# A four-layer model with routed experts on one core: where the first ranks' rows are added, and in which order layer 3's shared expert runs

## The chip, the cores and the metric

The kernel runs on one core of a Trainium2 chip. Five engines work from their own instruction queues: PE (matrix multiply), DVE (vector), ACT (scalar functions), POOL (general purpose) and SP (which here only issues transfers). They wait for each other with semaphores, and each executes its own queue in order. DMA queues move data between HBM and the on-chip memory. The metric is the device time of one execution in microseconds; the number quoted is a median over runs.

## The reference

The model has 1,024 tokens of width 256 (2 sequences of 512) in fp32 and four layers. Each layer is "macaron" shaped: half a feed-forward block, an attention-like block, half a feed-forward block. Layer 0 uses retention attention, layer 1 attention over selected tokens, layers 2 and 3 Mamba-2 blocks. The feed-forward blocks of layers 0 and 3 are mixtures of experts, and these are what the change touches:

```python
scores = softmax(x2d @ wg_router.T)                 # layer 3: sigmoid
topk_w, topk_idx = top_k(scores, TOP_K)             # layer 0: 6 of 32, layer 3: 2 of 8
...                                                 # layer 0: an expert takes at most C tokens
ye = (silu(xe @ w_gate) * (xe @ w_up)) @ w_down     # each expert on its tokens, F = 176
y = sum over the TOP_K ranks of ye * weight
sh = (silu(x2d @ ws_gate) * (x2d @ ws_up)) @ ws_down   # shared expert, on all tokens
return y + sh
```

Each token's result is a sum over its K chosen experts, plus the shared expert, plus the residual. Both blocks are run twice, before and after the layer's attention.

## The kernel before, in words

The tokens live on chip as `x`, eight chunks of 128 tokens (partitions) by 256. All four layers are one program. A tile framework places each engine's instructions by dependences; in some stretches the order is written out by hand with `in_order` (L230), which ties every instruction of the named engines to the one traced before it. `warm` (L254-259) issues PE matmuls whose result nobody reads, to fill PE's waits.

`moe` does a routed block. Its route (normalised tokens, router logits) may have been started by the stage in front; class `Route` has a method for each step (`measure`, `centre`, `turn`, `logit`, `load`, `clear`, `store`). Then:

- `choose` finds the top K experts of every token on DVE. `slots` (L531) gives each token a slot at each expert: a prefix count over tokens on PE (`ps_pos`, L540-541), then integer work on DVE (`sl_full` to `sl_hl`). `slot_lists` turns slots into two lists of row numbers, with one-hot tiles on DVE (L581-584) and PE, ended by a step `meet`: `sl_get` (which token to gather) and `sl_put` (where a result row goes).
- `shared_unit` (L472) runs the shared expert for one half of the tokens at a time: `front` multiplies by gate and up (L483), ACT makes silu, DVE multiplies (`h`, L487), `back` multiplies by down into `acc` (L493), and DVE adds `acc` to `x`. Layer 0 has three blocks of its hidden width, layer 3 two of 88.
- `experts_sparse` (L622) loops over experts in tiles of slots, software-pipelined over units: SP loads an expert's weights (L635-637) into one of five buffers of the pool `weights`; POOL gathers token rows (L645); PE transposes them (L661), multiplies by gate and up (L673); ACT and DVE form `he` (L677-678); PE transposes (L687), DVE or ACT copies to `hT`, PE multiplies by down (L698), DVE or ACT copies to `ye`, and POOL scatters `ye` to the array `rows` in HBM (L704). `rows` has K rows for every token, one for each rank; ranks follow the number of the expert, so a token's rank-0 row belongs to its first expert. A slot list hence fills rank 0 only from experts up to E-K, rank 1 only up to E-K+1, and so on.
- An overflow flag `over` decides whether further tiles are needed. All engines load it and branch around an `If` (L837-839); in these runs the body is not executed.
- After the `If`, every chunk needs its K rows. SP fetches them (L861) once all scatters have landed. `add` sums them: with a PSUM pool given, PE adds the K rows with identity matmuls (L879) and DVE adds the result (L880); else, for K=6, DVE adds rows 3-5 to rows 0-2 (L883, 128x768) and then three rows to `x` (L886); for K=2 two L886. These are not done by `moe` itself but left `pending` per chunk, and the stage that comes next calls `settle` (L261) for each chunk when it needs it. In layer 0's attention the order is written by hand, with `early_rows` making a chunk's addition fetch rows for the other half; in layer 1's front odd chunks of the first half and all of the second use PSUM.

Layer 3's routing is prepared in the stage in front: `l2_ffn2` ahead of its first routed block, the Mamba stage (steps near its end, from `NS - 7` on) ahead of its second.

Of the kernel before, what the change touches and what calls it, by code (L numbers as in the profile page):

```python
# [18 lines left out]
P = 128  # L19
# [82 lines left out]
class Route:  # L102

    def __init__(self, net, sb, xT, xn, pre, names, E, F, K, FS, PER, tiles, cap, r, scores, scale):
        self.net, self.sb, self.xT, self.xn = net, sb, xT, xn
        self.xns = [xn[c // CB][:, c % CB, :] for c in range(NC)]
        self.E, self.K, self.cap, self.r, self.scores = E, K, cap, r, scores
        a = net.a
# [10 lines left out]
        self.blocks, self.scales = None, {}  # L119
# [8 lines left out]
    def clear(self):  # L128
        nc = self.net.nc
        zero = self.sb.tile([P, D], F32, name="zero")  # L130
        nc.gpsimd.memset(zero, 0.0)
        for c in range(NC):
            nc.sync.dma_start(self.rv[c, :, : self.K, :], zero.unsqueeze(1).to_broadcast([P, self.K, D]))
# [38 lines left out]
    def store(self, b, engine):  # L172
        engine.dma_start(self.tv[b], self.xn[b])


class Net:
# [295 lines left out]
    def shared_unit(self, work, psA, psM, xT, blocks, half, scale):  # L472

        nc = self.nc
        cols = slice(half * S, (half + 1) * S)
        acc = [psA.tile([P, 2, D], F32, tag="acc", name=f"acc{i}") for i in range(2)]

        def front(gv, uv, bw):
            pg = psM.tile([P, S], F32, tag="mm", name="pg")
            pu = psM.tile([P, S], F32, tag="mm", name="pu")  # L480
            for ps, wv in ((pg, gv), (pu, uv)):
                for k in range(KD):
                    nc.tensor.matmul(ps[:bw], wv[:, k, :], xT[:, k, cols], start=(k == 0), stop=(k == KD - 1))  # L483
            s = work.tile([P, S], F32, tag="s", name="s")
            h = work.tile([P, S], F32, tag="h", name="h")
            nc.scalar.activation(s[:bw], pg[:bw], AF.Silu)
            nc.vector.scalar_tensor_tensor(h[:bw], s[:bw], scale, pu[:bw], ALU.mult, ALU.mult)  # L487
            return h

        def back(h, dv, bw, first, last):  # L490
            for tc_ in range(CB):

                nc.tensor.matmul(  # L493
                    acc[tc_ // 2][:, tc_ % 2, :],
                    h[:bw, tc_ * P : (tc_ + 1) * P],
                    dv,
                    start=first and tc_ % 2 == 0,
                    stop=last,
                    skip_group_check=True,
                )  # L500

# [247 lines left out]
    def moe(self, pre, names, E, F, K, FS, PER, tiles, cap, r, scores, scale):  # L749
# [6 lines left out]
        with ExitStack() as es:  # L756
# [4 lines left out]
            with ExitStack() as fs:  # L761
# [46 lines left out]
                for f in parts:  # L808
                    f()
# [1728 lines left out]
```

## Time and profile before

| quantity | us |
|---|---|
| median of 3 runs | 1982.44 (1980.68 to 1988.79) |
| the profiled execution, its own time | 1985.63 |
| its span | 1983.8 |
| PE busy | 1763.2 (89%) |
| DVE busy | 1148.7 (58%) |
| ACT busy | 817.4 (41%) |
| POOL busy | 924.2 (47%) |

The stages in the trace, in us from the start of the span: layer 0's first FFN 0-265, its attention 265-444, its second FFN 444-686; layer 1 686-869; layer 2 869-1140; layer 3's first FFN 1140-1250, its Mamba block 1250-1850, its second FFN 1850-1984.

A line of a timeline gives the start, the duration, the engine, the program line, the operation with the tiles it writes and reads, and in brackets how long the engine had been idle and who released it. A line of a table of windows gives the window, its length, and the busy time of PE, PE's weight loads, DVE, ACT and POOL in it, with instruction counts; then PE's granted clock, the share of DMA and the GB/s moved. An instruction of PE in fp32 appears as two pieces.

### The profile page before, as it was taken

The numbers are of one execution on the slowest core, as the hardware profiler recorded it, in microseconds if no ns is written. First come the engines' busy times: TensorE is split into PE (matmuls) and PEld (weight loads), VectorE is DVE, ScalarE is ACT, GpSimd is POOL, SyncE is SP. The second block draws the span as 40 slices with busy tenths as digits, with TensorE's granted clock in tenths as the row PEclk, the third lists the DMA queues.
The fourth block names the chain that finished last, engine by engine and source line by source line (L and its number), as shares of the span: only waits on it lengthen the run. The fifth ranks groups of instructions, "written<-read, shape, count | busy, mean of one in ns | idle before, by whom it ended". The sixth has DMA issues, their size and how long they took to land. (4 is left out here: it accounts for less than half of the span.)

```text
span 1983.8 us, 29591 instructions
## 1 busy us (share of the span) xinstructions
PE 1763.2 (89%) x10370; PEld 1249.3 (63%) x10370; DVE 1148.7 (58%) x2963; ACT 817.4 (41%) x1430; POOL 924.2 (47%) x946
## 2 busy tenths in 40 slices
PE   7988989998898887889788988789999999999985
PEld 4666766665666665554465456557777777777663
DVE  5422348346332367666676743578777877778523
ACT  1122225421222214421662112278877777777221
POOL 3556546522656440120142135136656656767362
PEclk8999999999999998999899999899999999999897
DMA  8355551052545360010130022534454544544132
GB/s 275 111 185 153 152 186 66 2 171 58 158 139 152 98 214 1 1 43 0 76 108 23 11 64 77 171 103 147 155 169 159 156 146 157 168 147 134 39 102 90
DMA packets 122216, 226.55 MB, mean 114 GB/s; under 512 B 22414, under 2 KB 75004, under 8 KB 121910
## 3 DMA queue, kind: packets, MB, share of 16 engines
q1 hardware_dynamic: 97062, 179.08, 27.9%
q0 software_dynamic: 18944, 42.16, 7.0%
q10 hardware_dynamic: 6032, 3.10, 0.6%
q8 instruction: 92, 1.51, 0.3%
q14 instruction: 86, 0.70, 0.1%
HBM read 195.59 MB, written 41.81 MB: 120 GB/s over the span
## 5 line engine op out<-in xcount | busy, mean ns | idle before, releaser
L645 POOL DMA_INDIRECT xe<-table,sl_get x176 | 181.0, 1029 | 206.3 <-DVE sl_get L617 96.6
L704 POOL DMA_INDIRECT rows<-ye,sl_put x176 | 176.8, 1004 | 126.4 <-DVE ye L225 40.9
L673 PE MATMUL ps_gu<-we,xeT 128*128 128x352 f32 x704 | 231.1, 470 | 1.6 <-DVE xeT L225 1.5
L698 PE MATMUL ps_ye<-we,hT 88*128 88x256 f32 x704 | 178.1, 395 | 38.6 <-issue 16.9
L698 PEld LDWEIGHTS ps_ye<-we,hT 88*128 88x128 f32 x704 | 135.0, 195 | 83.7 <-issue 20.4
L2066 DVE SCALAR_TENSOR_TENSOR xc<-pp,L_attn_cols,xc 128x511 f32<-128x511 f32 (+2 forms) x216 | 161.5, 748 | 26.2 <-ACT xc L2062 20.9
L678 DVE SCALAR_TENSOR_TENSOR he<-se,xe,ps_gu 128x176 f32<-128x176 f32 x176 | 68.3, 396 | 172.4 <-ACT se L677 93.5
L673 PEld LDWEIGHTS ps_gu<-we,xeT 128*128 128x128 f32 x704 | 129.7, 196 | 59.1 <-issue 4.8
L2181 DVE SCALAR_TENSOR_TENSOR lm<-lm,jb,top 128x128 f32<-128x128 f32 x576 | 153.6, 342 | 0.0
L2290 PE MATMUL yacc<-wt,y 128*128 128x256 f32 x576 | 142.7, 391 | 0.6 <-DVE x L2308 0.3
L2260 POOL TENSOR_TENSOR y<-y,sg 128x512 f32<-128x512 f32 x72 | 91.8, 1275 | 104.9 <-DVE y L2259 101.7
L677 ACT ACTIVATE se<-ps_gu 128x176 f32<-128x176 f32 x176 | 54.1, 318 | 204.7 <-PE ps_gu L673 117.9
L2205 PE MATMUL pz<-lateT,wt 128*128 128x128 f32 x1024 | 125.7, 276 | 6.2 <-ACT xt L2154 4.1
L2198 POOL TENSOR_TENSOR ce<-ce,CT 128x1024 f32<-128x1024 f32 x54 | 128.0, 2370 | 0.0
L2205 PEld LDWEIGHTS pz<-lateT,wt 128*128 128x128 f32 x1024 | 119.7, 192 | 9.3 <-ACT xt L2154 5.3
L2059 PE MATMUL pp<-lateT,wx 128*128 128x512 f32 x256 | 123.4, 605 | 1.4 <-DVE jb L2045 0.6
L1833 PE MATMUL ps_y<-w8T,xT 128*128 128x512 f32 x256 | 123.2, 610 | 0.0
L2233 PE MATMUL py<-lm,xt 128*64 128x128 f32 x1152 | 108.1, 281 | 14.4 <-ACT xc L2062 4.7
L2290 PEld LDWEIGHTS yacc<-wt,y 128*128 128x128 f32 x576 | 103.8, 190 | 22.7 <-issue 8.9
L2190 DVE TENSOR_TENSOR lm<-lm,M 128x1024 f32<-128x1024 f32 x72 | 87.2, 1215 | 45.6 <-ACT lm L2186 43.1
L2271 POOL TENSOR_TENSOR sqs<-sqs,sq 128x512 f32<-128x512 f32 x56 | 71.3, 1274 | 84.3 <-ACT sq L2270 84.3
L2221 POOL TENSOR_TENSOR xd<-xt,dec 128x512 f32<-128x512 f32 x54 | 56.4, 1044 | 93.5 <-ACT xt L2154 93.5
(510 smaller groups left out, 3562.6 us busy)
## 6 DMA issues: line engine op xcount, KB each, us to landing
lm<-rows SPq DMA_DIRECT2D x72, 512.0 KB
ce<-rows SPq DMA_DIRECT2D x54, 512.0 KB
y<-rows SPq DMA_DIRECT2D x16, 768.0 KB
we<-in_L_ffn_w_gate_dram SPq DMA_DIRECT2D x64, 176.0 KB
we<-in_L_ffn_w_up_dram SPq DMA_DIRECT2D x64, 176.0 KB
we<-in_L_ffn_w_down_dram SPq DMA_DIRECT2D x64, 176.0 KB
we<-in_L_ffn_w_dram SPq DMA_DIRECT2D x48, 176.0 KB
wx<-in_L_attn_in_proj_w_dram SPq DMA_DIRECT2D x16, 512.0 KB
```

The source lines that it names most:

```text
L645: nc.gpsimd.indirect_dma_start(xe[:, i, :], None, table, bass.IndirectOffsetOnAxis(get[:, at + j : at + j + 1], 0), bounds_check=T - 1, oo ...
L673: nc.tensor.matmul(pg, xeT[:, k, i * P : (i + 1) * P], wgu[:, :, k], start=(k == 0), stop=(k == KD - 1))
L698: nc.tensor.matmul(py[:, i, :], hT[:, q, i * P : (i + 1) * P], wd[:, q, :], start=(q == 0), stop=(q == 1))
L704: put_rows = nc.gpsimd.indirect_dma_start(rows, bass.IndirectOffsetOnAxis(put[:, at + j : at + j + 1], 0), y[:, i, :], None, bounds_check= ...
L1833: nc.tensor.matmul(ps, xT[:, k, :], self.w8T[:, k, 2 * e2 : 2 * e2 + 2, :], start=(k == 0), stop=(k == KD - 1))
L2059: nc.tensor.matmul(pp, wv[:, k, :], xT[:, k, b * S : (b + 1) * S], start=(k == 0), stop=(k == KD - 1))
L2066: nc.vector.scalar_tensor_tensor(out[:, 3 - w :], pp[:, : S - 3 + w], cw[:, m, w : w + 1], out[:, 3 - w :], ALU.mult, ALU.add)
L2181: nc.vector.scalar_tensor_tensor(k["lm"][:, h, :], k["lm"][:, h, :], jb[:, k["c"], n : n + 1], top, ALU.add, ALU.min)
L2198: nc.gpsimd.tensor_tensor(k["ce"], k["ce"], ct, ALU.mult)
L2205: nc.tensor.matmul(pz[:, m, :], u["wz"][:, kk, m * P : (m + 1) * P], xT[:, kk, c * P : (c + 1) * P], start=(kk == 0), stop=(kk == KD - 1),)
L2233: nc.tensor.matmul(py[i * HP : (i + 1) * HP, m, :], w[:, h * HP : (h + 1) * HP], v[:, h, :], start=(m == 0 and n == 0), stop=(n == len(src ...
L2290: nc.tensor.matmul(yacc[cc // 2][:, cc % 2, :], k["y"][:, m, :], u["wo"][:, m, :], start=(u["g"] == 0 and m == 0 and cc % 2 == 0), stop=(u ...
```

## The change

It has four parts.

1. **First ranks' rows are summed beside the last experts.** `early` is 4 of 6 ranks in layer 0, 1 of 2 in layer 3. When expert E-K+j is through (`done`), `take(j)` loads all tokens' rank-j rows (1 MB, in 1 KB pieces) by SP: rank 0 into a tile `sums` from the weight pool, later ranks into a single-buffered tile `yr`, which four DVE additions of 128x512 add to `sums`. Later scatters are declared independent of these loads, since later experts hold only higher ranks. After the `If`, four DVE additions of 128x512 add `sums` to `x`; the pending additions then fetch and add only the K-early last ranks. `early_rows` goes. L879 then runs for 2 rows instead of 6, L883 is gone.
2. **Rank 0 may now be read where nothing was scattered**, so for layer 3 `clear` is now called too, when the route is loaded: it writes zeros to the first rank's rows, in eight stores on SP, from a tile of zeros that POOL sets. The tile `latec` grows from 720 to 944 columns.
3. **The shared expert becomes a class `Shared`**, whose hidden tile `hs` is one buffer of the weight pool. Layer 3's front of half 0, block 0, is issued at the end of the stage in front (before the last chunk's `route_turn` in `l2_ffn2`; after `add_row` in the Mamba stage, with the shared weights loaded some steps before). Its second front takes the place of four warm matmuls in the second call, and stands behind `choose` in the first.
4. **Layer 3's lists get a fixed order** on PE and DVE: choose, slots (with the weighing of scores, `weigh`, between the prefix count's issue and `sl_full`), back and front of the next block, the list steps, two products `h`, `meet`, and then the rest of the shared expert.

The instruction order of the changed kernel, as built, puts the four additions of `take(1)` on DVE between the two `he` tiles of expert 30 in both calls of layer 0; those of `take(2)` and `take(3)` follow the last `hT`.

```diff
+        self.early = K - max(1, K // 3)
...
     def clear(self):
         nc = self.net.nc
+        n = self.K if self.cap < T else self.early
...
+            nc.sync.dma_start(self.rv[c, :, :n, :], zero.unsqueeze(1).to_broadcast([P, n, D]))
...
+class Shared:
+    def __init__(self, net, xT, blocks, scale):
+        self.hs = net.w("hs")[:, : B * len(blocks) * S].rearrange("p (b n t) -> p b n t", b=B, n=len(blocks))
+    def front(self, b, n, psum, pool, tag="s"):
...
+        nc.scalar.activation(s[:bw], pg[:bw], AF.Silu)
+        return partial(
+            nc.vector.scalar_tensor_tensor, self.hs[:bw, b, n, :], s[:bw], self.scale, pu[:bw], ALU.mult, ALU.mult
+        )
...
+                for other in self.taken:
+                    self.tc.declare_no_dep(put_rows.ins, other, reason="lower ranks than this expert can have")
                 self.puts.append(put_rows)
+            if done and js[-1] == tiles[-1]:
+                done(e)
...
-                        if left:
+                        if left and not route.shared_ahead:
                             self.warm(psM, 4)
+                        elif left:
+                            second = route.shared_ahead.front(0, 1, psM, work)
...
+                if shared:
+                    with self.in_order(tail, ("PE", "DVE")):
+                        for b in range(B):
+                            route.choose(b)
+                        if not left:
+                            second = shared.front(0, 1, psM, work)
+                        hl, row, full = self.slots(lists, sb, psL, mask, E, cap, r, weigh)
+                        shared.back(0, 0, psA)
+                        third = shared.front(1, 0, psM, work)
+                        where, parts = lists_of()
+                        for f in parts[:-1]:
+                            f()
+                        second()
+                        third()
+                        parts[-1]()
+                        third = shared.front(1, 1, psM, work)
+                        shared.back(0, 1, psA)
+                        shared.sum(0)
+                        third()
+                        for n in range(2):
+                            shared.back(1, n, psA)
+                        shared.sum(1)
...
+                def take(j):
+                    if j == 0:
+                        t = sums["of"]
+                    else:
+                        t = ew.tile([P, NC, D], F32, name="yr")
+                    nc.sync.dma_start(t, tv[j])
+                    self.taken.append(self.last_on("SP"))
+                    for c in range(0, NC if j else 0, 2):
+                        ac = sums["of"][:, c : c + 2, :]
+                        nc.vector.tensor_tensor(ac, ac, t[:, c : c + 2, :], ALU.add)
+
+                def done(e):
+                    j = e - (E - K)
+                    if j == 0:
+                        sums["of"] = self.w("sums")[:, : NC * D].rearrange("p (c d) -> p c d", d=D)
+                    if 0 <= j < early:
+                        take(j)
...
+        for c in range(0, NC, 2):
+            xc = self.x[:, c : c + 2, :]
+            nc.vector.tensor_tensor(xc, xc, sums["of"][:, c : c + 2, :], ALU.add)
...
         def add_rows(b, cc, psum):
+            n = K - early
+            for r in range(B):
+                if r not in ys and (r == b or cc == 0):
+                    ys[r] = self.w("y2")[:, : CB * n * D].rearrange("p (c n d) -> p c n d", c=CB, n=n)
+                    for i in range(CB):
+                        nc.sync.dma_start(ys[r][:, i], route.rv[r * CB + i, :, early:K, :])
+            y, xc = ys[b][:, cc], self.x[:, b * CB + cc, :]
+            if psum and n > 1:
...
             with self.in_order(tail, ("PE",)):
+                if route:
+                    shared.front(0, 0, psM, st)()
                 route_turn(NC - 1)
                 route_logit(NC - 1)
...
+                def begin():
+                    route.load()
+                    route.clear()
+                    route.shared_ahead = Shared(self, xT, self.load_shared(*route.shared), 0.5)
...
+            with self.in_order(tail):
+                project(ks.pop(NS - 1))
+                add_row(B - 1)
+                if not few:
+                    route.shared_ahead.front(0, 0, psM, wk, "sq")()
```

## The prediction

> **What bounds the kernel now.** I read the page's busy table first, then the stretches in which the diff acts, one at a time, in the timeline and the table of windows. The page:
>
> ```profile
> span 1983.8 us, 29591 instructions
> PE 1763.2 (89%) x10370; PEld 1249.3 (63%) x10370; DVE 1148.7 (58%) x2963; ACT 817.4 (41%) x1430; POOL 924.2 (47%) x946
> ```
>
> PE is busy for 89%, but this includes keep-warm matmuls, so a stage is judged by what it waits for. The change acts in six places: the two exits of layer 0's routed FFN (255-345, 670-735), the two heads of layer 3's (1138-1175, 1850-1887) and their two exits (1250-1264, 1966-1984). The first exit, on DVE (start, duration, instruction, idle before and its releaser):
>
> ```profile
> 254.58 0.40 DVE L678 SCALAR_TENSOR_TENSOR he<-se,xe,ps_gu 128x176 f32<-128x176 f32 x1 [0.85 <-ACT se L677]
> 255.76 0.40 DVE L678 SCALAR_TENSOR_TENSOR he<-se,xe,ps_gu 128x176 f32<-128x176 f32 x1 [0.79 <-issue]
> ...
> 262.12 0.69 DVE L225 COPY hT<-ps_he 88x512 f32<-88x512 f32 x1 [1.42 <-PE ps_he L687]
> 276.99 0.96 DVE L883 TENSOR_TENSOR y<-y 128x768 f32<-128x768 f32 x1 [14.18 <-DMA y<-rows]
> 277.98 1.34 DVE L886 TENSOR_TENSOR x<-x,y 128x256 f32<-128x256 f32 x3
> ```
>
> DVE is done with the experts at 262.8 and idles 14.18 us, until rows come back from HBM. Then every 128-token chunk costs a L883 and three L886, until 337. By then DVE is full (window, then busy PE, PEld, DVE, ACT, POOL):
>
> ```profile
> 310.00:321.00 11.00, 10.04 (x108) 7.24 (x107) 9.98 (x24) 5.59 (x16) 8.01 (x9) 1.00 0.25 77
> 321.00:332.00 11.00, 10.15 (x102) 6.68 (x101) 10.47 (x26) 6.41 (x19) 8.34 (x9) 1.00 0.08 26
> 332.00:343.00 11.00, 10.99 (x111) 7.62 (x110) 9.93 (x24) 5.11 (x16) 7.79 (x9) 1.00 0.17 51
> ```
>
> Layer 3's first head, on PE:
>
> ```profile
> 1142.69 0.69 PE L148 MATMUL pt_r<-cst,laten 128*128 128x128 f32 x2 [4.49 <-DVE laten L307]
> 1143.84 1.02 PE L154 MATMUL ps_lg<-latec,lateT 128*128 128x8 f32 x4 [0.46 <-ACT lateT L149]
> 1145.12 3.71 PE L483 MATMUL pg<-lateT,wsh 128*88 128x512 f32 x4 [0.26 <-DVE latec L157]
> 1148.63 2.82 PE L483 MATMUL pu<-lateT,wsh 128*88 128x512 f32 x4
> 1151.28 1.02 PE L483 MATMUL pg<-lateT,wsh 128*88 128x512 f32 x2
> 1152.14 0.34 PE L540 MATMUL ps_pos<-sl_pre,cst 128*128 128x72 f32 x2
> ```
>
> PE idles 4.49 us, runs cold afterwards (0.85 us a piece; granted clock 0.50 in 1145-1150), and reaches the slot count (ps_pos) at 1152.14, behind ten shared-expert pieces, though DVE had its input by 1148.1. The last exit, on DVE:
>
> ```profile
> 1969.25 1.68 DVE L886 TENSOR_TENSOR x<-x,y 128x256 f32<-128x256 f32 x4 [10.16 <-DMA y<-rows]
> 1971.61 0.89 DVE L886 TENSOR_TENSOR x<-x,y 128x256 f32<-128x256 f32 x2 [0.69 <-DMA y<-rows]
> 1972.70 1.68 DVE L886 TENSOR_TENSOR x<-x,y 128x256 f32<-128x256 f32 x4 [0.20 <-DMA y<-rows]
> 1975.89 0.88 DVE L886 TENSOR_TENSOR x<-x,y 128x256 f32<-128x256 f32 x2 [1.50 <-DMA y<-rows]
> 1978.68 1.68 DVE L886 TENSOR_TENSOR x<-x,y 128x256 f32<-128x256 f32 x4 [1.91 <-DMA y<-rows]
> ```
>
> 6.8 us of adds take 11.1 us, because fetches reuse buffers and stand behind output stores on SP.
>
> **First exit of layer 0.** Added: four takes of 1 MB in 1 KB pieces, 12 adds of 128x512 into sums, 4 into x. An add is taken at 0.69 us (L883 moves 768 columns in 0.96), four at 2.8. A take: attention weights of the same piece size moved at about 345 GB/s (250-253), so 3.0 us, plus some 2 for start and landing (a 256 KB row fetch issued at 1252.14 let DVE start at 1254.83): 5.0. Bounds: 3.0 (transfer alone) to 7.
>
> In the changed instruction order DVE meets the first four adds between expert 30's two he tiles, and they need take 1. That take waits for expert 27's second scatter (issued 249.29; its packets end by 252-253) and lands at about 257.5; the adds end at 260.4, so the he of 255.76 starts 4.6 us late. Queued behind it are he and hT of experts 30 and 31, and behind those PE's down projections and POOL's last four scatters, whose last (267.06) goes about 2 us late, because PE now runs expert 31's gate/up inside the gap. All takes after the first share one buffer yr: take 2 runs 260.5-265.5, its adds end at 268.3; take 3 lands at 273.4, its adds end at 276.2. Then DVE reads the overflow flag, branches and fetches code: before, its branch stood at 262.76 and its next record at 265.62, which cost nothing ahead of the 14 us wait; now these 3.4 us are in the chain: 279.6. Four adds into x: 282.4; two row adds: chunk 0 is complete at 283.2 rather than 279.3. The row fetch itself (landing near 277-278) is hidden behind this chain. So +3.9 at the start.
>
> [...]
>
> Chunks 0 to 7 lose L883 (8.4 us in this window) and a third of L886 (15.3): 13.5 us of DVE, of which 2.3 belong to chunks 0 and 1 and are returned at once, the rest in steps where DVE is 9.9-10.5 of 11 busy, but PE 10.0-11.0 too. Ends: 0 (PE bounds) and 11.2 (DVE alone). I take 6, since PE's busy time includes cold and modelled ends. Sum: +3.9 -2.3 -6 = **-4** (range +4 to -9). SP's five weight loads move from 247 to behind take 1 (253); first used after 283, so free.
>
> **Second exit, and layer 1's front.** The same chain: take 1 lands at 676, adds to 678.5, he late by 3.6, last scatter +0.8; take 2's adds 685.8, take 3's 693, branch 696.4, adds into x 699.2, chunk 0 at 700.0, against 698.7: +1.3. After it, L883 of chunks 0 and 2 (1.0 and 1.4 us) and two L886 (0.9) go; of 36 row matmuls 24 go, two PE passes each. PE's share is largely hidden: from 716 to 730 a chunk takes 4.5 us of DVE with two POOL round trips and PE waits for DVE. But at 702.3-706.2 PE waits 3.9 us for chunk 1 and then runs cold twelve passes at 0.43 instead of 0.22. I credit -3.3 for DVE and -2 for this: **-4**, ends 0 and -8.
>
> **Layer 3's heads.** First: one front (8 pieces of 0.43 = 3.4 us) moves into PE's 4.49 us idle before 1142.69. The next front runs warm beside the choosing, so ps_pos comes at about 1148.7 instead of 1152.1: **-3.4**, carried by the one-hots, sl_get (1164.07) and the first gather. Ends: 0 (clock still cold, or lists late) and -5. Second: ps_pos at 1866.68 stands behind fronts, its input ready about 1863.2; sl_hl gains 0.8 more because h no longer precedes it; front (0,1), replacing the warm matmuls, may delay the transposes of 1855.46 by 0.9: **-3.3**, ends 0 and -5. Each call adds one table load (1.28 us, as at 1143.80); ACT idles 1134.0-1143.4 and 1849.8-1857.6, so free, and 1.28 each without that cover. Outside that cover two loads would cost 2.6. [...]
>
> Clearing: eight more stores on SP twice, 0.4 us of issue each, 3.2 together, in front of lm/ce loads that waited 5.0-8.7 us around 1797-1815, and early in layer 2's FFN where SP has nothing queued; POOL gains one 128x256 memset. Free; 3.2 without cover. The hs tile takes one of five weight buffers; expert loads are paced by PE, so free. The earlier weighing fills DVE's wait for ps_pos.
>
> **Layer 3's exits.** SP's release (after the branch and POOL's last scatter) stays. Its one take waits for expert 6's scatter; its landing, DVE's branch (1244.62, 1959.16) and four adds of 2.8 us end before rows land (1254.8, 1969.2). First: 128 KB rather than 256 KB a fetch (-0.4), one add less for four chunks (4 x 0.45): **-2**, ends 0 and -3; the wx weights stand behind eight fetches instead of four, 1.3 us of issue. Last: eight fetches issue without waiting, 1966.65 to 1970; the last row lands near 1972.2, added by 1972.7; SP issues the eight stores from 1970.4 at 0.4 each: last about 1973.3 rather than 1980.38: **-7**, ends -4 and -8.
>
> **Sum.** -4 -4 -3.4 -3.3 -2 -7 = -23.7 us on the profiled execution (1985.63; span 1983.8, 1.8 around it). That run stands 3.2 over the median 1982.44, so 1961.9 there, 1958.7 against the median: **1959**, -1.2%.
>
> **Rivals.**
> - Takes longer than 5 us (mixed with weight loads and scatters), say 7: three in a row, +6 per exit of layer 0, +12: 1971. For: one yr buffer. Against: little other traffic there (33-130 GB/s after 253).
> - Heads stay, because lists and gathers, not PE order, set the first expert: +6.7: 1966. For: 5 us of one-hots on DVE after the count. Against: these follow ps_pos directly.
> - Slower: DVE's in-order wait for takes dominates both exits. Every us over 5 adds 3 at each exit, 6 in all: break-even at 9 us, and takes of 11 us give -23.7 + 36 = +12: 1995. For: 4 extra MB read per call while scatters write the same rows. Against: 11 us would mean about 115 GB/s where 345 was seen.
> - Nothing measurable: PE bounds layer 0's attention, the starts are late and only the last store moves: about 1977.
>
> **How the numbers follow.** Forecast (1945-1968) 0.58; long takes 0.13; heads unmoved 0.11; slower 0.08; nothing 0.10. All ends of the layer 0 gains together reach 1946; range 1944-1980, the forecast's own 1945-1968. About 0.5%, 10 us, is what a measurement can tell. The first three cases are faster (0.82, less 0.04 for long takes beyond 7 us): faster 0.78; same 0.13; slower 0.09.
>
> **What would show it.** The first adds on sums waiting for a take with he right behind them; chunk 0 of layer 0's attention 3-5 us late after the exit and its DVE windows below 9.5 of 11; ps_pos 3 us after the logits; no L886 waits at the end. Wrong if the takes land later than 6 us, PE keeps its step in layer 0's attention, or code fetching costs more.

## The result: slower by half a per cent

The changed kernel took 1991.66 us (median of 22 runs, 1984.36 to 2007.22); the kernel before, run beside it, 1984.69 us. The ratio is 1.0048, with a 95% interval of 1.0027 to 1.0068: about 9.5 us slower (the medians alone differ by 7.0), where the forecast was 23.7 us faster, and outside the range. The profiled execution of the changed kernel was one of its shortest, 1984.82 us. Its page:

```profile
span 1982.9 us, 29549 instructions
PE 1756.4 (89%) x10314; PEld 1242.5 (63%) x10314; DVE 1152.0 (58%) x2967; ACT 821.7 (41%) x1432; POOL 931.1 (47%) x948
```

The span is 0.8 us *shorter* than before's, which hides what happened. The table splits both spans at instructions that both kernels have (starts read off the two traces; after minus before):

| stretch | us |
|---|---|
| layer 0, first exit: expert 26's first scatter to chunk 0's normed rows (39.56 to 45.56) | +6.0 |
| layer 0's attention (to its second routing's last logit) | -2.8 |
| layer 0, second exit (38.17 to 44.99) | +6.8 |
| layer 1's front | -1.2 |
| layer 1's attention, and layer 2's two FFNs and block | +4.9, +4.3 |
| layer 3, first head: last `w8T` matmul to first scatter (47.22 to 46.37) | -0.9 |
| layer 3, first exit (17.37 to 18.11) | +0.7 |
| layer 3, second head: last norm sum (`pr`) to first scatter (51.08 to 50.59) | -0.5 |
| layer 3, last exit: last scatter to last store (18.50 to 13.26) | -5.2 |
| the four expert loops, and the start up to the first gather | -12.4 |

The last row is chance: from expert 1's first scatter to expert 26's, layer 0's first loop takes 152.1 us in this trace, 156.1 in before's and 157.2 to 163.5 in the traces of the first two series below, and the change touches nothing in it before its end. Without it the stretches add up to +12, which is in line with the measured +9.5. So layer 0's exits lose 12.8 us, the gains of layer 3 are mostly missing, and another 9 us in layers 1 and 2, which no run here explains, come on top (last paragraph of the account below).

**The first exit.** DVE's timeline of the changed kernel (start, duration, instruction, idle before and releaser), to be held against the lines of before in which both `he` follow each other at 254.58 and 255.76:

```profile
246.21 0.40 DVE L687 SCALAR_TENSOR_TENSOR he<-se,xe,ps_gu 128x176 f32<-128x176 f32 x1 [0.85 <-ACT se L686]
251.74 2.50 DVE L893 TENSOR_TENSOR sums<-sums,yr 128x512 f32<-128x512 f32 x4 [5.13 <-DMA w<-in_L_attn_q_w_dram]
254.15 0.70 DVE L687 SCALAR_TENSOR_TENSOR he<-se,xe,ps_gu 128x176 f32<-128x176 f32 x2
...
260.83 2.48 DVE L893 TENSOR_TENSOR sums<-sums,yr 128x512 f32<-128x512 f32 x4
269.69 2.50 DVE L893 TENSOR_TENSOR sums<-sums,yr 128x512 f32<-128x512 f32 x4 [6.38 <-SPq L915]
273.49 2.50 DVE L936 TENSOR_TENSOR x<-x,sums 128x512 f32<-128x512 f32 x4 [1.31 <-DVEq L915]
275.91 0.88 DVE L954 TENSOR_TENSOR x<-x,y 128x256 f32<-128x256 f32 x2
```

DVE stands still between expert 30's two `he` for 5.13 us and then adds for 2.50: the second `he` is 7 us late. (The releaser named is a weight load; at the second exit the same wait of 4.90 us is put down to `yr`.) PE and POOL of the same kernel show how far that reaches:

```profile
248.68 1.35 PE L682 MATMUL ps_gu<-we,xeT 128*128 128x352 f32 x4
254.60 0.88 PE L696 MATMUL ps_he<-cst,he 128*88 128x128 f32 x3 [4.57 <-DVE he L687]
255.27 2.55 PE L682 MATMUL ps_gu<-we,xeT 128*128 128x352 f32 x4
```

```profile
250.92 0.99 POOL L713 DMA_INDIRECT rows<-ye,sl_put  x1 [0.30 <-issue]
260.64 0.98 POOL L713 DMA_INDIRECT rows<-ye,sl_put  x1 [8.73 <-ACT ye L275]
261.93 2.25 POOL L713 DMA_INDIRECT rows<-ye,sl_put  x1 [0.30 <-issue]
...
265.77 0.98 POOL L713 DMA_INDIRECT rows<-ye,sl_put  x1 [0.30 <-issue]
```

PE runs half of expert 31's gate/up pieces (four, 1.35 us, granted clock 1.00) inside the gap, waits 4.57 us for DVE, and then needs 2.55 us for the other four, at half rate (granted clock 0.50). POOL waits 8.73 us for `ye`. One of its scatters then takes 2.25 us instead of 0.98; it runs beside DVE's additions of take 2 (260.83 to 263.31). Of the 2464 scatters in the 14 traces here eleven take 2.0 to 3.5 us, and each of these lies beside such additions into `sums`. The last scatter comes 31.0 us after expert 26's first, against 23.9 before; 0.6 of these 7.1 us are the slow scatter's.

**Layer 0's attention.** The three windows of DVE's fullest stretch, moved by the microsecond by which the stage starts later (busy PE, PEld, DVE, ACT, POOL, then clock, DMA):

```profile
311.00:322.00 11.00, 10.61 (x119) 7.48 (x112) 7.69 (x21) 6.20 (x20) 7.77 (x9) 1.00 0.01 1
322.00:333.00 11.00, 10.37 (x121) 6.86 (x113) 8.58 (x21) 5.30 (x15) 7.87 (x10) 1.00 0.01 3
333.00:344.00 11.00, 10.61 (x113) 7.48 (x110) 6.64 (x19) 6.09 (x18) 7.42 (x9) 1.00 0.01 1
```

DVE fell from 9.9-10.5 of 11 to 6.6-8.6, as forecast. PE stayed at 10.4-10.6: it bounds the stretch, and the stage shortened by 2.8 us only.

**Layer 3's first head and last exit**, on PE and on DVE:

```profile
1148.41 0.61 PE L156 MATMUL ps_lg<-latec,lateT 128*128 128x8 f32 x4 [0.46 <-ACT lateT L151]
1149.28 3.47 PE L192 MATMUL pg<-lateT,wsh 128*88 128x512 f32 x4 [0.26 <-DVE latec L159]
1152.58 1.88 PE L192 MATMUL pu<-lateT,wsh 128*88 128x512 f32 x4
1154.30 0.34 PE L547 MATMUL ps_pos<-sl_pre,cst 128*128 128x72 f32 x2
```

```profile
1970.14 2.50 DVE L936 TENSOR_TENSOR x<-x,sums 128x512 f32<-128x512 f32 x4 [6.00 <-DVEq L915]
1975.09 1.88 DVE L954 TENSOR_TENSOR x<-x,y 128x256 f32<-128x256 f32 x4 [2.45 <-DMA y<-rows]
1977.21 0.83 DVE L954 TENSOR_TENSOR x<-x,y 128x256 f32<-128x256 f32 x2 [0.23 <-DMA y<-rows]
1978.35 0.79 DVE L954 TENSOR_TENSOR x<-x,y 128x256 f32<-128x256 f32 x2 [0.32 <-DMA y<-rows]
```

`ps_pos` comes 5.9 us after the logits instead of 8.3, but the front that was to run warm runs its first four pieces at half rate (3.47 us at a granted clock of 0.53, against 1.88 at 1.00 for the next four). At the end the waits between the row additions are gone, as forecast.

### The profile page after: what moved, and what is told of

Read it like the earlier page. It is cut to its first block, busy times and chain, and to the rows that moved or that the text cites. A ratio compares the mean times of both kernels' runs of the same rounds, so it can differ in the third digit from the quotient of the medians.

```text
span 1982.9 us, 29549 instructions
## 1 busy us (share of the span) xinstructions
PE 1756.4 (89%) x10314; PEld 1242.5 (63%) x10314; DVE 1152.0 (58%) x2967; ACT 821.7 (41%) x1432; POOL 931.1 (47%) x948
## 5 line engine op out<-in xcount | busy, mean ns | idle before, releaser
L654 POOL DMA_INDIRECT xe<-table,sl_get x176 | 185.6, 1055 | 183.8 <-DVE sl_get L626 91.0
L713 POOL DMA_INDIRECT rows<-ye,sl_put x176 | 181.3, 1030 | 141.7 <-ACT ye L275 54.0
L707 PE MATMUL ps_ye<-we,hT 88*128 88x256 f32 x704 | 175.7, 391 | 37.7 <-issue 12.2
L2266 POOL TENSOR_TENSOR ce<-ce,CT 128x1024 f32<-128x1024 f32 x54 | 128.1, 2373 | 0.0
```

The source lines that it names most:

```text
L654: nc.gpsimd.indirect_dma_start(xe[:, i, :], None, table, bass.IndirectOffsetOnAxis(get[:, at + j : at + j + 1], 0), bounds_check=T - 1, oo ...
L707: nc.tensor.matmul(py[:, i, :], hT[:, q, i * P : (i + 1) * P], wd[:, q, :], start=(q == 0), stop=(q == 1))
L713: put_rows = nc.gpsimd.indirect_dma_start(rows, bass.IndirectOffsetOnAxis(put[:, at + j : at + j + 1], 0), y[:, i, :], None, bounds_check= ...
L2266: nc.gpsimd.tensor_tensor(k["ce"], k["ce"], ct, ALU.mult)
```

## The experiments

They ran in three series, each on one chip beside the kernel before: 1995.40 us there in the first, 1993.60 in the second, 1899.96 in the third, on a chip that runs this program 5% faster. Ratios are compared across series, microseconds inside one.

### First series: which part costs?

**Layer 0 undone, layer 3 kept.**

```diff
-        self.early = K - max(1, K // 3)
+        self.early = K - max(1, K // 3) if K == 2 else 0    # with before's fetch and add for K == 6
```

> The changed kernel with layer 0 as before (all six ranks fetched after the branch, no takes); layer 3's early rank and the new order of its shared expert stay. Stall theory (the loss sits at layer 0's two exits, where DVE stops behind take 1 and the takes follow each other through one buffer; in the two traces these exits with the stage behind them lose 3.5 and 5.5 us): 9 us below the changed kernel, about 2 to 6 below before (ratio 0.997 to 0.999). Clock theory (the loss sits in stages that the change does not touch, because PE is granted a lower clock there): still about 5 to 7 above before (1.003). Order theory (the fixed order of layer 3's lists costs more than it gives): about even with before (1.000).

Measured: 1987.76 us, ratio 0.9964 (0.9938 to 0.9989).

**Layer 3's heads as before, early ranks kept in both layers.**

```diff
-            shared = route.shared_ahead = Shared(self, route.xT, self.load_shared(*route.shared), 0.5)
+            route.blocks = self.load_shared(*route.shared)
...
-                    shared.front(0, 0, psM, st)()
```

> The changed kernel with layer 3's shared expert and lists in the order of before; the early ranks of both layers stay. Stall theory: the heads are worth nothing, so it stays within 2 us of the changed kernel (ratio to before 1.003 to 1.005). Order theory: 4 us or more below the changed kernel, and the first expert of layer 3's second call starts 2 to 3 us earlier after the Mamba stage's last matmul than in the changed kernel. Clock theory: as the changed kernel.

Measured: 2003.45 us, ratio 1.0040 (1.0014 to 1.0067).

**Layer 3's early rank alone** (both edits).

> Layer 3's early rank alone: layer 0 as before, layer 3's shared expert and lists in the order of before. All theories but the clock theory: 6 to 8 us below before (ratio 0.996 to 0.997), from the last exit. Beside the run with the new order of layer 3: equal in the stall theory, 3 us or more lower in the order theory. Clock theory: above before like the changed kernel.

Measured: 1992.21 us, ratio 0.9979 (0.9951 to 1.0007).

What follows: layer 0's early ranks make the difference between the last two, 11.2 us, and they are the whole loss. Layer 3's early rank is worth some 3 us (its interval reaches 1), and the interval of rank and head order together stays below 1. What the head order adds by itself isn't shown: the first and the last of these kernels differ by 4.5 us with overlapping intervals, the second (1.0040) and the changed kernel (1.0048, in another series) by nothing, and in the traces the two heads together are 1.3 to 1.8 us shorter.

**The additions traced behind the last expert**, with a tile of its own for take 2, and take 3 behind take 1's additions.

```diff
-                    for c in range(0, NC if j else 0, 2):
-                        ac = sums["of"][:, c : c + 2, :]
-                        nc.vector.tensor_tensor(ac, ac, t[:, c : c + 2, :], ALU.add)
+                    sums[j] = t                # take 2: self.w("yr2"); take 3 behind take 1's additions
...
                 self.experts_sparse(ew, psE, xes, *args[0], where, *args[1], tiles, beside, done=done)
+                add_up()
```

> The changed kernel, in which layer 0's additions of takes 1 to 3 are issued after the last expert, with a second buffer (from the weight pool) for take 2; nothing else. Stall theory: he and hT of experts 30 and 31 keep their pace of before (last scatter about 5 us earlier than in the changed kernel), sums is complete about as early, chunk 0 of layer 0's attention 4 to 6 us earlier at each exit: 8 to 10 us below the changed kernel, ratio to before 0.998 to 1.000. If the chain of takes and the branch set the end rather than the stalled experts: under 3 us below the changed kernel. Clock theory: no difference.

Measured: 2010.72 us, ratio 1.0065 (1.0037 to 1.0092), and exits of 51.9 and 48.5 us. DVE's timeline says why this was no test of the stall:

```profile
264.08 0.69 DVE L899 TENSOR_TENSOR sums<-sums,yr 128x512 f32<-128x512 f32 x1 [5.51 <-DMA yr<-rows]
264.69 0.39 DVE L687 SCALAR_TENSOR_TENSOR he<-se,xe,ps_gu 128x176 f32<-128x176 f32 x1
...
286.30 2.50 DVE L899 TENSOR_TENSOR sums<-sums,yr 128x512 f32<-128x512 f32 x4 [12.13 <-SPq L924]
```

The framework, which orders by dependences, still put the first addition between the two `he`. What the edit did add is a take 3 that is issued later and whose additions start only at 286.30: a longer chain costs too, even when the stall is the same.

### Second series: the stall, the chain, and the heads

**One early rank in layer 0**: one take straight into `sums`, no addition before the branch.

```diff
+        self.early = K - max(1, K // 3) if K == 2 else 1    # rows 1 to 5 then come back with the chunks, by pairs
```

> Layer 3 as in the changed kernel; in layer 0 only one rank is taken early (one take, straight into sums, no addition on DVE before the overflow branch; five rows per token come back with the chunks). Theory A (the takes that DVE waits for in order, and their one-after-the-other chain, cost the time): both exits of layer 0 as in the kernel before (from expert 26's scatter to chunk 0's normed rows 39.5, to the final norm 38), the whole at 0.994 to 0.998 of before, about the kernel with layer 0 undone (0.9964). Theory B (reading the rows beside the scatters, or a later loss in layers 1 and 2, costs it): a part of the loss stays, 2 to 5 us per exit or in layers 1 and 2, ratio 1.000 or above.

Measured: 1986.58 us, ratio 0.9967 (0.9945 to 0.9989); exits 38.6 and 37.7.

**Two early ranks** (`else 2`): take 1's additions stand between the `he` tiles, takes 2 and 3 don't exist.

> Layer 3 as in the changed kernel; in layer 0 two ranks are early. Take 1's four additions stand between expert 30's two he tiles on DVE as in the changed kernel, but takes 2 and 3 are gone. Theory A in the form that the stall alone sets the loss: DVE waits about 5 us for take 1, the last scatter comes 6 to 7 us late and both exits are 45 and 44 us as in the changed kernel, ratio 1.002 to 1.005. Theory A in the form that the chain of takes 2 and 3 sets it: exits 40 and 38.5, ratio 0.995 to 0.999. Between: the scatters are late by 6.6 and the exits by 3 to 5.

Measured: 1993.71 us, ratio 1.0005 (0.9980 to 1.0030); exits 42.1 and 43.3. DVE:

```profile
252.05 0.40 DVE L687 SCALAR_TENSOR_TENSOR he<-se,xe,ps_gu 128x176 f32<-128x176 f32 x1 [0.85 <-ACT se L686]
256.92 2.50 DVE L893 TENSOR_TENSOR sums<-sums,yr 128x512 f32<-128x512 f32 x4 [4.47 <-SPq L915]
259.33 0.70 DVE L687 SCALAR_TENSOR_TENSOR he<-se,xe,ps_gu 128x176 f32<-128x176 f32 x2
```

**Three early ranks, the eight additions ordered on DVE behind expert 31's last work.**

```diff
                 self.experts_sparse(ew, psE, xes, *args[0], where, *args[1], tiles, beside, done=done)
+                with tc.issue_after(self.last_on("DVE")):
+                    add_up()
```

> Layer 3 as in the changed kernel; in layer 0 three ranks are early, takes 1 and 2 each have a tile of their own, and their eight additions are ordered behind expert 31's last work on DVE. Theory A: DVE idles nothing at expert 30, the last scatter is where it was before, the additions run from about 263 to 268 while the scatters finish, sums are in x by 274 and the rows, not the chain, set chunk 0: exits 38 to 40, layer 0's attention 1 to 3 us shorter, ratio 0.993 to 0.997. Theory B (traffic, or later losses): exits 43 or more, or layers 1 and 2 longer by 5, ratio 1.000 or above.

Measured: 1984.93 us, ratio 0.9972 (0.9951 to 0.9993); exits 41.1 and 39.6. DVE:

```profile
253.11 0.40 DVE L687 SCALAR_TENSOR_TENSOR he<-se,xe,ps_gu 128x176 f32<-128x176 f32 x1 [0.85 <-ACT se L686]
254.29 0.40 DVE L687 SCALAR_TENSOR_TENSOR he<-se,xe,ps_gu 128x176 f32<-128x176 f32 x1 [0.79 <-issue]
...
261.25 2.48 DVE L899 TENSOR_TENSOR sums<-sums,yr 128x512 f32<-128x512 f32 x4
264.28 2.55 DVE L899 TENSOR_TENSOR sums<-sums,yr 128x512 f32<-128x512 f32 x4 [0.55 <-DMA yr<-rows]
271.86 0.69 DVE L945 TENSOR_TENSOR x<-x,sums 128x512 f32<-128x512 f32 x1 [5.03 <-DVEq L923]
```

The exits of these kernels, each split at the last scatter's issue and at SP's first fetch of rows (us, first exit / second exit):

| kernel | expert 26's first scatter to the last | to the row fetch | to normed rows | sum |
|---|---|---|---|---|
| before | 23.9 / 23.9 | 5.1 / 5.7 | 10.5 / 8.5 | 39.6 / 38.2 |
| changed | 31.0 / 31.7 | 6.4 / 6.4 | 8.2 / 6.9 | 45.6 / 45.0 |
| one rank | 23.9 / 23.9 | 4.8 / 5.4 | 9.8 / 8.4 | 38.6 / 37.7 |
| two ranks | 28.1 / 29.8 | 5.1 / 5.8 | 9.0 / 7.7 | 42.1 / 43.3 |
| three, held behind the experts | 24.6 / 26.6 | 7.4 / 5.7 | 9.2 / 7.4 | 41.1 / 39.6 |

This settles where layer 0's exits lose. One addition group between the `he` tiles makes the last scatter 4.2 and 5.8 us late, by itself; with takes 2 and 3 behind it, 7.1 and 7.8. Without it the scatters are in time (one rank) or late by 0.6 and 2.6 (held). These last two have another cause: the slow scatter beside DVE's additions, which takes 2.25 us at the first exit and 3.53 at the second, in the held kernel as in the changed one; of the changed kernel's 7.1 and 7.8 it accounts for 0.6 and 1.9. After the fetch the early ranks gain 0.1 to 2.3 us, of which the changed kernel loses 1.2 and 0.7 again before it. So the loss comes from where the additions stand: with one rank, which puts none there, it is gone, and the exits are 1.0 and 0.5 us shorter than before. That one rank gains in the whole isn't shown (0.9967, against 0.9964 with layer 0 undone on another chip).

The first exit of the kernel with three ranks held is still 1.7 us longer than with layer 0 undone: the row fetch came 7.4 us after the last scatter there, where it was 4.9. DVE idled 5.03 us at its branch, but that isn't what held the chunk: its additions into `x` ended at 275.9, 2.6 us before the first row addition (278.5). SP had been standing at its wait for the scatters' landing since 4.2 us after the last scatter, and POOL, which reports it, waited until 5.4.

**Layer 3's heads mended**, layer 0 as before: PE alone in fixed order, the second call's first front in the routed stage with its product `hs` behind the layernorm, the second front behind the choosing in both calls.

```diff
-                    route.shared_ahead.front(0, 0, psM, wk, "sq")()
...
-                            second = route.shared_ahead.front(0, 1, psM, work)
+                            first = route.shared_ahead.front(0, 0, psM, work)      # first() behind the layernorm
...
-                    with self.in_order(tail, ("PE", "DVE")):
+                    with self.in_order(tail, ("PE",)):
```

> Layer 0 as before. Layer 3's early rank as in the changed kernel; in its heads the fixed order holds PE alone, not DVE, the second call's first front comes in the routed stage with its product behind the layernorm, and the second front stands behind the choosing in both calls. Theory (DVE's fixed order and the hs product ahead of the layernorm's statistics ate the gain of the heads): each head's path from the last state product to the first scatter is 1 to 2.5 us shorter than with the fixed order (46.8 and 52.0 us with it), and the whole 2 to 5 us under the kernel with layer 0 undone, ratio 0.993 to 0.996. Rival (PE's shared-expert pieces behind the lists, run at half rate, set the first expert): the lists are ready sooner, the first scatter is not, and the ratio stays at 0.9964 within 0.0015.

Measured: 1981.10 us, ratio 0.9939 (0.9914 to 0.9964), the lowest here. The first head gained nothing (46.9 us): its first gather came 24.2 us after the last `w8T` matmul, against 25.1 with one rank in the same series, whose first scatter came at 46.8 all the same. The second gained 4 to 5 (46.9 instead of 50.6 in the changed kernel and 52.0 with layer 0 undone). Some of these 4 to 5 us are luck: with the same heads in the third series the second head's first gather came as early (26.6 and 27.6 us after the last norm sum, 26.7 here, 29.9 to 31.9 in the other kernels), but its first scatter at 49.7 and 47.7; in the first of these PE ran two groups of four pieces behind the lists at half rate (3.72 and 3.11 us). So the gain up to the gather repeats, the one up to the scatter only in part. DVE, where the layernorm's statistics start, in the changed kernel and in this one:

```profile
1856.41 1.66 DVE L2376 SCALAR_TENSOR_TENSOR x<-yacc,rs,x 128x256 f32<-128x256 f32 x4
1859.65 0.68 DVE L2550 SCALAR_TENSOR_TENSOR hs<-s,pu 88x512 f32<-88x512 f32 x1 [1.58 <-ACT s L196]
1860.37 0.75 DVE L365 BATCH_NORM_STATS2 ln_st<-x 128x6 f32<-128x256 f32 x2
```

```profile
1854.21 1.66 DVE L2411 SCALAR_TENSOR_TENSOR x<-yacc,rs,x 128x256 f32<-128x256 f32 x4
1855.95 0.75 DVE L365 BATCH_NORM_STATS2 ln_st<-x 128x6 f32<-128x256 f32 x2
```

### Third series: which piece of the heads, and can the parts be joined?

**Only DVE freed**: as the first kernel of all, with `("PE",)` in the place of `("PE", "DVE")` and both first fronts where the change has them.

> Layer 0 as before; layer 3 as in the changed kernel, but the fixed order of the choosing and the lists holds PE alone, not DVE; both first fronts stay where the change has them. Theory 1 (the fixed order on DVE cost the second head's gain): the first gather of the second call comes 27 us after the last norm sums as with the mended heads (26.7; 30.5 to 31.9 with the fixed order), ratio 0.994 to 0.995. Theory 2 (the hs product in front of the layernorm's statistics and the second front in front of its transposes cost it): 29 to 31 us, ratio 0.996.

Measured: 1891.92 us, ratio 0.9973 (0.9955 to 0.9991). The second call's first gather came 30.1 us after the last norm sums, not 27: theory 2 holds for the second head. Its first head was short, 43.5 us, though that kernel's program and the mended one's say the same there. PE's lines of this kernel and of the two-rank kernel below (46.3 us) show the first difference:

```profile
1075.35 1.95 PE L192 MATMUL pg<-lateT,wsh 128*88 128x512 f32 x4 [0.26 <-DVE latec L159]
1077.14 1.88 PE L192 MATMUL pu<-lateT,wsh 128*88 128x512 f32 x4
1078.86 0.41 PE L547 MATMUL ps_pos<-sl_pre,cst 128*128 128x72 f32 x2
```

```profile
1066.26 3.50 PE L192 MATMUL pg<-lateT,wsh 128*88 128x512 f32 x4 [0.26 <-DVE latec L159]
1069.59 1.88 PE L192 MATMUL pu<-lateT,wsh 128*88 128x512 f32 x4
1071.31 0.34 PE L547 MATMUL ps_pos<-sl_pre,cst 128*128 128x72 f32 x2
```

Whether four pieces behind a short wait run at full or half rate decides 1.5 us of the 2.8; 0.3 more lies in half-rate list pieces, 1.0 behind the first gather.

**One early rank in layer 0, and the mended heads.**

> One early rank in layer 0 together with layer 3's heads with PE alone in fixed order. If the parts add up: layer 0's exits as in the one-rank kernel (38.6 and 37.7), its attention 2 to 4 us shorter than before, layer 3 as in the other (first gather of the second call about 27 us after the last norm sums), together 2 to 5 us under the kernel with layer 3's heads alone (0.9939): ratio 0.991 to 0.995. If they don't add: 0.994 or above.

Measured: 1888.21 us, ratio 0.9946 (0.9925 to 0.9967).

**Two early ranks in layer 0, additions behind expert 31, and the mended heads.**

> As the kernel with one early rank in layer 0, but two ranks are early, and take 1's four additions stand behind expert 31's last work on DVE. Theory (the additions cost only by where they stand): no wait at expert 30, additions done by 265 while the last scatters land, exits 38 to 39.5, one row less per chunk, ratio 0.990 to 0.994. Rival (one more 1 MB take in front of the weight loads delays scatters and code loading as with three ranks, where the exits were 41.1 and 39.6): exits 40 and more, ratio 0.993 to 0.997.

Measured: 1889.44 us, ratio 0.9948 (0.9925 to 0.9970). Exits 36.6 and 34.0 us (one rank: 37.3 and 33.5; layer 0 as before, on this chip: 37.8 and 36.3), so the additions cost next to nothing there (the last scatter came 0.6 to 0.9 us later). The gains do not add up beyond the mended heads' 0.9939: the three kernels can't be told apart, and all three beat both kernels.

**Three early ranks held, the next stage's weight loads behind the branch.**

```diff
-            self.prepare_next([normed] * new + [self.loaded[E // 4]] * (self.calls <= 2))
...
+        if K > 2:                                # behind the If
+            self.prepare_next([normed] * new + [self.loaded[E // 4]] * (self.calls <= 2))
```

> As the kernel with three early ranks held behind expert 31, but the five 256 KB weight loads of the next stage stand behind the overflow branch on SP instead of in front of it. There SP's code came 8 us after its branch, DVE's next record 5 us after its own, and the row fetches 7.4 us after the last scatter's issue (4.8 with one rank). Theory (2.3 MB of take and weights in the queues delays the last scatters and the code): SP and DVE go on 3 to 5 us after their branches, the rows are fetched 5 us after the last scatter, exit 1 is 38 to 39.5. Rival (the delay belongs to the branch and the scatters themselves): exit 1 stays at 41, or longer with the loads in front of the row fetches. The whole: within 3 us of 0.9972.

Measured: 1900.17 us, ratio 1.0001 (0.9985 to 1.0018): 5.5 us worse than expected from 0.9972. At the first exit SP's first transfer behind its branch came 5.9 us after it, where the held kernel had none before 8.0, and DVE idled 3.05 us before its first addition there instead of 5.03. That fits loads that delay the code, but doesn't show it: the two kernels ran on different chips, and at the second exit SP stood until 8.5 us after its branch without the loads in front. The row fetch still came 6.8 us after the last scatter (SP had stood at its wait since 2.7, POOL had the landing at 4.9), and the exits were 38.2 and 37.1, 0.3 and 0.8 us longer than with layer 0 as before on that chip. Where the rest of the ratio went, the traces don't settle: its profiled run of 1893.35 us is 7 us below its median.

## Why the prediction was wrong

**First exit of layer 0 (-4, measured about +3): the step that failed** is "whose last (267.06) goes about 2 us late, because PE now runs expert 31's gate/up inside the gap". The wait, its place and the instructions queued behind it were right, and the delay of the second `he` (4.6 forecast) was 7: take 1 needed 5.7 us from its issue (246.03) to DVE's start rather than 5.0, and was issued 1.4 us ahead of that `he`'s usual place, not 3.3. The recovery was not there: only half of the gate/up fitted into the gap and the other half ran at half rate (2.55 us instead of 1.35), so that expert 31's last `he` was still 6.3 us late; the slow scatter beside take 2's additions added 0.6, and the last scatter was 7.1 us late. Two ranks alone already show 4.2; there the second half ran at full rate, and 1.9 us of 6.1 were recovered.

**The chain of takes** was mis-sized less: take 3 was issued at 263.3 and its additions began at 269.7, 6.4 us against 5.0. The branch was in the chain but cheap: DVE reached it at 270.53, ahead of its own additions' end, and its additions into `x` began 1.31 us after them, where 3.4 was put in. From branch to next record DVE needs 2.8 us here, as in before (262.83 to 265.62). In each of these stretches the two DMA queues that the trace lists as instruction queues moved one packet each, 0.02 and 0.01 MB, which fits the forecast's fetch of code; that DVE waited for just these two isn't shown. At the first exit with three ranks held, where 2.3 MB of take and weights are under way, DVE needs 6.6 and SP 8.0. At layer 3's exits DVE's next record came 2.8 us after its branch in before and 5.1 to 7.8 us after it in the 13 kernels that have a 1 MB take under way there; no run has the one without the other. What mattered was how much of it ran beside other work.

**The attention after it** (-8.3 for fewer additions, measured -2.8): of the ends "0 (PE bounds) and 11.2 (DVE alone)" the first was nearly the truth, and the 6 taken had no row behind it but a doubt about PE's busy time. The windows show PE at 10.4-10.6 of 11 once DVE is free.

**Second exit and layer 1's front (-4, measured +5.6)**: the same failed step (+0.8 forecast for the last scatter, +7.8 measured); the gain in layer 1's front was 1.2 instead of 5.3, so most of the rows that PE and DVE no longer add must have been hidden. (The forecast's "All ends of the layer 0 gains together reach 1946" takes -9 and -8 for -4 and -4, which gives about 1950; the range is not touched by it.)

**The slower rival** named the right mechanism, DVE's in-order wait for takes at both exits, and a wrong price: "every us over 5 adds 3 at each exit", break-even at takes of 9 us. With takes of 5.6 to 7.0 us it had already won, because the forecast's base of 5 us was itself costed at a scatter 2 us late.

**Layer 3's heads (-3.4 and -3.3, measured -0.9 and -0.5).** In the first, `ps_pos` did come earlier (5.9 us after the logits instead of 8.3), and the first gather 3.0 us earlier (24.1 us after the last `w8T` matmul instead of 27.1). The step that failed is "carried by the one-hots, sl_get (1164.07) and the first gather": the gather doesn't set the first expert. PE's first product there, `ps_xe`, stands behind the shared expert's last pieces, 8.5 us after the first gather before (1164.36 to 1172.82) and 11.9 in the changed kernel (1166.16 to 1178.09). Before, then after:

```profile
1167.39 3.62 PE L493 MATMUL acc<-wsh,h 88*128 88x256 f32 x16
1172.82 0.63 PE L661 MATMUL ps_xe<-cst,xe 128*128 128x128 f32 x4
```

```profile
1162.32 1.81 PE L602 MATMUL ps_sl<-sl_ol,sl_oh 128*32 128x64 f32 x64 [2.25 <-DVE sl_oh L593]
1165.12 3.72 PE L192 MATMUL pg<-lateT,wsh 128*88 128x512 f32 x4
...
1170.75 5.53 PE L208 MATMUL acc<-wsh,hs 88*128 88x256 f32 x24
1178.09 0.63 PE L670 MATMUL ps_xe<-cst,xe 128*128 128x128 f32 x4
```

What the front saved in PE's 4.49 us of idle time went into waits of 2.25 and 0.73 us in front of the lists' products, where there were none before, and into pieces at half rate behind them. The rival "heads stay" thus named the right result and, with PE's order, the wrong reason.

In the second, `ps_pos` came 1.0 us later, counted from the last norm sum. "ps_pos at 1866.68 stands behind fronts, its input ready about 1863.2" was wrong (ready at 1864.4), and putting DVE in a fixed order too cost more: the layernorm's statistics began 2.30 us after `x` was complete, behind the product `hs`, and 0.08 us where `hs` stands behind them; and from the logits to the count's input DVE needed 5.6 us instead of 4.4. The table load called free was off by 0.25 us only: `hs` waited for the silu, which ended at 1859.62, but also for `pu`, which PE had at 1859.37. Every one of the 110 loads in the changed kernel's trace takes 1.28, and the silu behind this one starts 0.01 us after it.

**Layer 3's exits (-2 and -7, measured +0.7 and -5.2).** "SP's release (after the branch and POOL's last scatter) stays" failed by little: the take stands in front of the branch on SP, so SP branched 3 to 4 us ahead of the last scatter instead of 31 to 36, and the first row fetch came 6.6 and 6.1 us after that scatter instead of 4.9 and 4.8. The twelve other kernels with that take show 5.5 to 7.1. The late branch is not the cause: SP stood at its wait 3.6 and 1.7 us after the last scatter, long before the fetch. POOL, which reports the scatters' landing, did so 1.7 and 1.3 us later than before. The take's megabyte was under way at both exits, but no run without it tells whether it is the cause. The gain from fetches without buffer waits was as forecast.

**Not forecast and not settled**: layer 1's attention and layer 2 took 9 us more in the changed kernel's trace. Part is chance: layer 1's attention takes 107.0, 107.3 and 109.4 us in kernels with layer 0 as before, and the long ones have a lower granted clock in the same stretch (0.66-0.79 in 788-808 of the changed kernel). But the six traces of the first two series and the changed kernel with early ranks in layer 0 lie at 108.9 to 111.7 there, and five of them at 68.9 to 70.1 in layer 2's first FFN, against 67.4 in all without. It isn't tied to early ranks alone: on the third series' chip layer 1's attention takes about 107, 107 and 109 us in the three kernels with early ranks and 109 in the one without, and layer 2's first FFN 67.4 in all four. No run here tells why.

## What to carry to other kernels

An instruction that waits for a transfer must not be placed between two links of a chain that another engine is waiting for, however idle its own engine is: here what stood behind it in DVE's queue came late by nearly the whole wait and its work (5.13 and 2.50 us; the second `he` 7 us late), and the chain paid most of that (the last scatter 7.1 us late, 0.6 of it the slow scatter's; with two ranks 4.2 of 6.1). Count none of it as recovered unless a row shows work that really fills the gap. Look at the built order of each engine, and tie such work behind the last link explicitly; tracing it later is not enough. And before crediting a relieved engine, read what the next one has left in the same window: DVE went from about 10 to 7.6 of 11 us and the stage gained 2.8 us, because PE stood at 10.5.

## What the runs showed of the hardware

Layer 0's first expert loop takes 128.0 to 128.1 us in the four kernels of the third series, whose chip is faster, and 152 to 163 in all other traces, with the same instructions. The table of windows shows where, on PE (window, busy PE, PEld, DVE, ACT, POOL, clock, DMA share, GB/s), first before's and then those of the third series' two-rank kernel:

```profile
130.00:170.00 40.00, 32.77 (x210) 24.09 (x210) 11.39 (x26) 8.20 (x20) 22.97 (x23) 1.00 0.50 145
170.00:210.00 40.00, 36.77 (x162) 28.57 (x163) 12.07 (x24) 9.30 (x23) 26.61 (x27) 0.91 0.48 148
```

```profile
130.00:170.00 40.00, 40.00 (x194) 31.57 (x194) 14.66 (x29) 12.10 (x28) 30.85 (x31) 1.00 0.61 185
170.00:210.00 40.00, 40.00 (x194) 31.57 (x193) 14.66 (x29) 12.10 (x28) 30.10 (x30) 1.00 0.60 187
```

On the faster chip PE works without a gap at full clock. Elsewhere it idles in between (before, 130-210: 6.9 us in two waits in front of `ps_ye` that the trace puts down to no other engine) and is granted 0.91 at times. What makes it wait wasn't found.

The half-rate pieces behind a short wait are not a property of the instruction order: the same order gave 1.95 and 3.50 us for the same four pieces after the same 0.26 us of idle. In the changed kernel's first head the granted clock was 0.53 over four such pieces (3.47 us) and 1.00 over the next four (1.88 us). What sets it there isn't shown, so a forecast of such a stretch should carry both values.

A scatter beside DVE's 128x512 additions of fetched rows took 2.0 to 3.5 us on POOL instead of 0.98 in eleven cases, and nowhere else in these traces; why isn't shown.
